# Four graph layers on one core: the ends of layer 3 rearranged, and their statistics and row scalings given to ScalarE

## The chip, the cores and the metric

The kernel runs on one core of a Trainium2 chip. A core has engines that run side by side, each with its own queue of instructions: TensorE (PE in the profile; loads of its weights are PEld) for matrix products, VectorE (DVE) for elementwise work and reductions, ScalarE (ACT) for functions of one argument, GpSimd (POOL), and SyncE (SP), whose queue issues most transfers. SBUF holds working data in 128 partitions; PSUM takes TensorE's results. The metric is the device time of one execution in microseconds (us), lower is better.

## The reference, cut to what matters

Input x is 16 batches of 1024 nodes with 64 features; adj is one 1024 x 1024 0/1 matrix for all batches. Four layers follow each other, each as a residual with a layer norm:

```python
x = _layernorm(x + _L0_gnn_ref(x, W, a, adj))              # attention with additive scores
x = _layernorm(x + _L1_gnn_ref(x, w0, b0, wa, ba, adj))    # softmax per feature over neighbours
x = _layernorm(x + _L2_gnn_ref(x, adj, W, a))              # as layer 0
x = _layernorm(x + _L3_gnn_ref(x, adj, Wh, bh, Wo, bo, gamma, beta))

# layer 3
mask = graph + eye(N) > 0
h = einsum('bnc,hdc->bhnd', x, Wh)                 # 4 heads of 64
scores = where(mask, einsum('...nd,...md->...nm', h, h), NEG)
out_h = softmax(scores) @ h + bh
z = leaky_relu(cat(out_h), 0.2)                    # 256 features
h2 = z @ Wo.T                                      # 64 features: the outer attention
out2 = softmax(where(mask, h2 @ h2.T, NEG)) @ h2 + bo
z2 = leaky_relu(out2, 0.2)
out = (z2 - mean) * rsqrt(var + 1e-5) * gamma + beta
```

So layer 3 ends, for each batch, in two layer norms: the inner one with gamma and beta, and the one of the residual.

## The kernel before

The nodes lie in 128 partitions times 8 chunks (C = 8). Layers 0 to 2 pass over the batches in turn. In layer 3 each batch has 32 **head units** and 8 **outer units**. A unit is one key chunk against 1024 queries: scores on TensorE into a PSUM tile, their exponential on ScalarE into a tile e, the mask on VectorE (e times the adjacency), the product of e with the values on TensorE. Head units work on two of the four heads at once (lines 1330 to 1354), pair n = 0 first and then n = 1, each with query halves h = 0 and 1. Outer units (lines 1486 to 1524) work on the single outer head; for them VectorE also adds up the masked rows (`add_up`, line 1499), except in the last batch, where `add_all` (line 1526) does it by matmuls with ones.

The units are grouped into **bursts** of five (`plan`, line 1998, and `run`, line 2011). Batch b has bursts 0 to 7; a burst holds five head units in bursts 0 to 3, and in bursts 4 to 7 three head units of b with two outer units of b - 1 between them. Batches are counted from 0 to 15, E = 15 is the last. For every burst `run` writes, in this order: finishing steps left over (`catch_up`), the scores and exponentials of its five units, the tasks listed under `mids`, the roots of pending variances (`roots`, on ScalarE), the products of the burst before (`drain`), the masks of this burst, the tasks listed under `slots`. The order on TensorE, ScalarE, VectorE and GpSimd is the order written (`manual_schedule`); SP's queue is ordered by the framework. Score tiles rotate through three PSUM buffers (`ps_s`); other PSUM results in layer 3 take turns in the same three. There are eleven buffers for e.

Tasks are put at (batch, burst) by `at`. The list at line 1917 places what follows the head units of a batch: projection of a pair's result (`project_T`), the reciprocal of its sums, which go through DRAM by SP's queue (`inverse`), the quotient and leaky ReLU (`quotient`); then the outer projection (`h_2T`, line 1443), the bound of its scores (`shift_of`, line 1268: norms by TensorE, maximum by VectorE, across partitions by GpSimd, to ScalarE's bias), its values (`h_2v`). After a batch's outer units come its **ends** (lines 1548 to 1666): `gather` turns the result and divides it by its sums, `layer` adds bo and applies the leaky ReLU, `mean`, `centre` and `scale` make the inner norm from sums, differences, squares and sums of squares over full-width tiles (128x512), all on VectorE; `affine` multiplies by the inverse root and gamma, `residual` adds beta and x, three more steps make the second norm, `finish` scales and stores. Roots are taken on ScalarE (logarithm and exponential, line 706) and improved by a step of three small VectorE instructions (line 710). Batch 14 takes its powers on GpSimd, its second squares on ScalarE (line 1636) and its last scaling row by row on ScalarE.

Elsewhere there is another form: `bn_stats` (eight instructions), `moments` (line 754: seven small instructions, then root, step and shift) and `scaled` (line 776), which scales eight chunks, one ScalarE instruction each:

```python
for c in rows:
    nc.scalar.activation(dst[:, c, :], src[:, c, :], AF.Identity,
        bias=shift[:, c : c + 1], scale=rstd[:, c : c + 1])
```

Layer 2 ends its batches so (`store`, line 1112). Its tasks have places of their own (lines 1130 to 1141); those at or after step `own` of the round behind its last batch are carried into the bursts of layer 3's batch 0, one per burst. In the round itself stand the eviction of the last batch's product, its projection, the division and, ahead of them, row scalings of batches 12 and 13.

After the last head units comes a serial stretch: the second pair of batch 15 is projected and divided (`project`, line 1399), turned (`z_T`, line 1437), projected (`h_2T`), and the 8 outer units of batch 15 run as burst 8; then sums, the quotient and two norms (`last_layer`, `last_quotient`, `last_norms`). Ten checks of value bounds (`known`, line 2033, `look`, line 2042) are written into this stretch; if a check fails a general path runs.

Of the kernel before, what the change touches and what calls it, by code (L numbers as in the profile page):

```python
# [8 lines left out]
F32 = mybir.dt.float32  # L9
# [7 lines left out]
P = 128  # L17
# [565 lines left out]
def fast_path(  # L583
# [316 lines left out]
    def gat_layer(w, name, zero_mean, own, room=None):  # L900
# [238 lines left out]
        for b in range(B):  # L1139
            for task, (t, k) in zip(work[b][2], ends[b % 2]):  # L1140
                at(b + t, k, task)
# [293 lines left out]
    def prep_out(b):  # L1435

        def z_T():
            pt = ps_s.tile([P, C, P], F32, tag="s", name="pzT")
            for c in range(C):
                nc.tensor.transpose(pt[:, c, :], zs[b][:, c, :], ident)  # L1440
            nc.scalar.copy(zTs[b][:, NP - 1, :], pt.rearrange("p c q -> p (c q)"))

        def h_2T():
# [5 lines left out]
            pt = one_bank("ph2T")  # L1449
            for n in range(NP):  # L1450
                for h in range(2):
                    nc.tensor.matmul(  # L1452
                        pt[h * D : (h + 1) * D, :], woT[:, n], zTs[b][:, n, h * HALF : (h + 1) * HALF],
                        start=(n == 0), stop=(n == NP - 1),
                    )
# [25 lines left out]
        return z_T, h_2T, h_2v, swap, biased  # L1481

    def head_out(b):
# [42 lines left out]
        def add_all():  # L1526
            t = ps_h.tile([P, HALF], F32, tag="acc0", name="u2")
            for k in range(C):
# [5 lines left out]
            held["u"] = l3.tile([P, HALF], F32, tag="y", name="u2T", bufs=1)  # L1534
            nc.scalar.copy(held["u"], t)

        def turned():
# [7 lines left out]
            held["tot"] = po[1][:, : 2 * CH].rearrange("p (j h) -> p j h", h=2)  # L1545
# [15 lines left out]
        def last_quotient():  # L1561
            total = sums[:, b, H, :]
            for j in range(CH):
# [44 lines left out]
        def layer():  # L1608
# [4 lines left out]
            held["n"] = normalizing(v, held["m"], b >= B - 2)  # L1613
# [6 lines left out]
        def residual():  # L1620
            m = held["m"]
            if b < B - 2:
                nc.vector.tensor_tensor(m, m, bc_mid(beta, C), ALU.add)
            nc.vector.tensor_tensor(m, m, xb(b), ALU.add)
            held["n"] = normalizing(m, held["v"], b >= B - 2)
# [10 lines left out]
        def squares():  # L1636

            m, sq = held["m"], held["v"]
            st = small.tile([P, C], F32, tag="ln_sum", name="ln_sum")
            nc.vector.tensor_reduce(st, m, AX.X, ALU.add)  # L1640
            held["less"] = small.tile([P, C], F32, tag="ln_mean", name="ln_mean")
            nc.vector.tensor_scalar(held["less"], st, -1.0 / D, None, ALU.mult)
            held["vs"] = small.tile([P, C], F32, tag="ln_vs", name="ln_vs")
            for c in range(C):
                nc.scalar.activation(
                    sq[:, c, :], m[:, c, :], AF.Square, bias=held["less"][:, c : c + 1],
                    accum_out=held["vs"][:, c : c + 1],
                )

        def power():  # L1650
            ve = small.tile([P, C], F32, tag="ln_ve", name="ln_ve")
            nc.vector.tensor_scalar(ve, held["vs"], 1.0 / D, LN_EPS, ALU.mult, ALU.add)
            held["rstd"] = small.tile([P, C], F32, tag="ln_rstd", name="ln_rstd")
            nc.gpsimd.tensor_tensor(held["rstd"], ve, neg_half, ALU.pow)

        def rows():
            shift = small.tile([P, C], F32, tag="ln_ve", name="ln_shift")
            nc.vector.tensor_tensor(shift, held["less"], held["rstd"], ALU.mult)
            res = ep.tile([P, C, D], F32, tag="m", name="res", bufs=4)
            scaled(res, held["m"], (held["rstd"], shift), range(C))  # L1660
# [10 lines left out]
        ends = [gather, layer, mean, centre, scale, affine, residual, mean, centre, scale, finish]  # L1671
# [434 lines left out]
```

## Time and profile before

| | |
|---|---|
| median of 3 runs | 1978.29 us (1972.04 to 1978.98) |
| profiled execution | 1970.04 us, span 1967.8 us |
| mean granted TensorE clock | 0.984 |
| busy: TensorE, VectorE, ScalarE, GpSimd | 1879.4, 1762.7, 1332.3, 83.0 us |
| layer 3: first scores, first scores of batch 1 | 649.75, 715.70 us |
| first scores of batch 14, of batch 15 | 1749.26, 1828.91 us |
| last mask of a head unit ends | 1918.9 us |
| outer masks of batch 15 | 1933.0 to 1942.2 us |
| first statistics of batch 15's norms | 1952.73 us |

Times are from the start of the span. A row of the order-of-time view gives start, duration, engine, line, operation, output and input tiles, shapes and count of merged instructions; in brackets the idle time before it and what ended that. A row's duration of several merged instructions is from the first start to the last end. "Granted clock" is the share of full speed that the throttle left to TensorE.

### The profile page before, as it was taken

How to read it: one execution, taken by the hardware profiler on the slowest of the kernel's cores; microseconds unless marked ns; L12 is line 12 of the kernel's file. 1: busy time of each engine (PE TensorE's matmuls, PEld its weight loads, DVE VectorE, ACT ScalarE, POOL GpSimd, SP SyncE). 2: the span in 40 equal slices, each digit the busy share in tenths (PEclk: the TensorE clock that was granted, in tenths of full speed). 3: DMA queues.
4: the chain of work that ended last, by engine and by line, in shares of the span. 5: the costliest groups of instructions: out<-in, count | busy, mean ns of one | idle time of the engine just before them, and what ended most of it. 6: DMA issues, size and time to landing. Idle time of an engine off the chain costs nothing.

```text
span 1967.8 us, 25841 instructions
## 1 busy us (share of the span) xinstructions
PE 1879.4 (96%) x9545; PEld 767.6 (39%) x9545; DVE 1762.7 (90%) x2963; ACT 1332.3 (68%) x2344; POOL 83.0 (4%) x77
## 2 busy tenths in 40 slices
PE   7999989989888899999999999999999999999985
PEld 4444437863333333333333333333333333333332
DVE  5899988879999777798999989999899898998997
ACT  5356567857667776667767767677666776776653
POOL 0000000000000000000000000000000000000001
PEclk8999999999999999999999999999999999999998
DMA  7000000000000120000000000000000100010000
GB/s 179 1 1 1 1 1 1 1 1 1 1 1 3 51 56 12 12 12 19 22 17 12 20 25 12 17 18 22 17 12 18 28 12 17 12 28 17 12 17 18
DMA packets 45748, 35.90 MB, mean 18 GB/s; under 512 B 37295, under 2 KB 37616, under 8 KB 45614
## 3 DMA queue, kind: packets, MB, share of 16 engines
q1 hardware_dynamic: 45310, 34.14, 6.7%
q8 instruction: 77, 1.26, 0.3%
q14 instruction: 57, 0.47, 0.1%
q10 hardware_dynamic: 304, 0.03, 0.0%
HBM read 29.45 MB, written 4.70 MB: 17 GB/s over the span
## 4 chain that ended last, share of the span: by engine, by line
PE 70%; DVE 22%; ACT 5%; issue 1%; DMA 1%; POOL 0%; SPq 0%; DVEq 0%; POOLq 0%; ACTq 0%
PE y L1351 19%; PE s L1336 19%; DVE e L991 7%; PE y_l L1003 6%; PE po L1833 5%; PE y L1516 4%; PE s L1491 4%; DVE e L1344 4%; PE u_l L1015 3%; DVE e L1509 2%; DVE junk L1501 1%; PE phT L1310 1%; ACT e L1340 1%; PE poT L1378 1%; PE ph2T L1452 1%
## 5 line engine op out<-in xcount | busy, mean ns | idle before, releaser
L1340 ACT ACTIVATE e<-s,shift 128x1024 f32<-128x1024 f32 x512 | 539.3, 1123 | 221.2 <-PE s L1336 221.2
L1344 DVE TENSOR_TENSOR e<-e,aT 128x1024 f32<-128x1024 f32 x512 | 596.4, 1215 | 12.9 <-ACT e L1340 12.9
L1336 PE MATMUL s<-hT 64*128 64x512 f32 x2048 | 491.6, 604 | 1.4 <-ACT hT L1319 0.9
L1351 PE MATMUL y<-e,vals 128*64 128x512 f32 x2048 | 485.6, 601 | 5.5 <-DVE e L1344 4.3
L991 DVE SCALAR_TENSOR_TENSOR e<-G_l,q,aT 128x1024 f32<-128x1024 f32 x256 | 315.4, 1275 | 6.4 <-ACT G_l L968 6.3
L1336 PEld LDWEIGHTS s<-hT 64*128 64x128 f32 x2048 | 183.5, 186 | 289.0 <-issue 149.6
L1003 PE MATMUL y_l<-e,vals_l 128*64 128x512 f32 x1024 | 254.2, 616 | 26.9 <-DVE e L991 20.1
L1351 PEld LDWEIGHTS y<-e,vals 128*64 128x64 f32 x2048 | 135.9, 137 | 273.5 <-issue 200.3
L1509 DVE TENSOR_TENSOR e<-e,aT 128x1024 f32<-128x1024 f32 x128 | 156.2, 1225 | 9.8 <-DVE junk L1501 0.5
L1501 DVE SCALAR_TENSOR_TENSOR junk<-e,aN 128x1024 bf16<-128x1024 f32 x120 | 146.1, 1218 | 0.0
L1496 ACT ACTIVATE e<-s,shift 128x1024 f32<-128x1024 f32 x128 | 138.4, 1114 | 0.4 <-PE s L1491 0.4
L1516 PE MATMUL y<-e,h2v 128*64 128x512 f32 x512 | 127.2, 599 | 0.9 <-DVE e L1509 0.9
L1491 PE MATMUL s<-h2T 64*128 64x512 f32 x512 | 125.8, 591 | 0.0
L1003 PEld LDWEIGHTS y_l<-e,vals_l 128*64 128x64 f32 x1024 | 62.3, 138 | 160.4 <-issue 75.7
L1833 PE MATMUL po<-hi,aR 128*128 128x512 f32 x256 | 102.7, 402 | 11.1 <-ACT hi L1762 7.3
L1279 POOL PARTITION_ALL_REDUCE gtop<-top x48 | 55.3, 1152 | 1268.7 <-DVE top L1277 970.0
L1833 PE MATMUL po<-lo,aR 128*128 128x512 f32 x256 | 101.0, 395 | 0.0
L780 ACT ACTIVATE x<-m,bn_shift,bn_rstd 128x64 f32<-128x64 f32 x256 | 88.5, 430 | 0.0
L1491 PEld LDWEIGHTS s<-h2T 64*128 64x128 f32 x512 | 50.0, 186 | 60.2 <-issue 37.3
L1383 ACT COPY zT<-poT 64x512 f32<-64x512 f32 x124 | 72.0, 581 | 1.3 <-PE poT L1378 0.2
L1516 PEld LDWEIGHTS y<-e,h2v 128*64 128x64 f32 x512 | 36.6, 138 | 76.4 <-issue 58.5
L978 ACT ACTIVATE vals_l<-x,p 128x64 f32<-128x64 f32 (+1 forms) x256 | 64.3, 339 | 0.0
(270 smaller groups left out, 1876.1 us busy)
## 6 DMA issues: line engine op xcount, KB each, us to landing
r<-inverse SPq DMA_DIRECT2D x62, 256.0 KB
adj<-in_adj_dram SPq DMA_DIRECT2D x16, 512.0 KB
x<-in_x_dram SPq DMA_DIRECT2D x16, 256.0 KB
out_dram<-res SPq DMA_DIRECT2D x15, 256.0 KB
rows<-yT SPq DMA_DIRECT2D x62, 4.0 KB
sums<-rows SPq DMA_DIRECT2D x31, 8.0 KB
inverse<-rt SPq DMA_DIRECT2D x31, 8.0 KB
out_dram<-res SPq DMA_DIRECT2D x2, 128.0 KB
```

Source lines behind the costliest of these rows:

```text
L991: nc.vector.scalar_tensor_tensor(e, G[b - b % 2][:, b % 2, :], pq[b - b % 2][1][:, k, b % 2 : b % 2 + 1], aT[:, k, :], ALU.max, ALU.mult,)
L1003: nc.tensor.matmul(held["y"][h * D : (h + 1) * D, :], vals[b][:, k, :], e[:, h * HALF : (h + 1) * HALF], start=(k == 0), stop=(k == C - 1),)
L1336: nc.tensor.matmul(s[:, i, :], hT[rows, k * P : (k + 1) * P], hT[rows, cols], start=True, stop=True)
L1340: nc.scalar.activation(e, s, AF.Exp, bias=shifts[b, n])
L1344: nc.vector.tensor_tensor(e, e, bc_mid(aT[:, k, h * HALF : (h + 1) * HALF], 2), ALU.mult)
L1351: nc.tensor.matmul(held[h][i * D : (i + 1) * D, :], vals[b][:, k, :], e[:, i, :], start=(k == 0), stop=(k == C - 1),)
L1491: nc.tensor.matmul(s[:, i, :], hT[rows, (i + k // CH) % 2, k % CH * P : (k % CH + 1) * P], hT[rows, 0, :], start=True, stop=True,)
L1496: nc.scalar.activation(e, s, AF.Exp, bias=shifts[b])
L1501: nc.vector.scalar_tensor_tensor(junk.rearrange("p c q -> p (c q)").bitcast(BF16), e.rearrange("p i q -> p (i q)"), 1.0, aN[:, k, :], ALU. ...
L1509: nc.vector.tensor_tensor(e, e, aT[:, k, :].rearrange("p (i q) -> p i q", i=2), ALU.mult)
L1516: nc.tensor.matmul(held["o"][h * D : (h + 1) * D, :], vals["out", b][:, k, :], e[:, h, :], start=(k == 0), stop=(k == C - 1),)
L1833: nc.tensor.matmul(po.rearrange("p q k f -> p (q k f)"), aR[:, k, ic * P : (ic + 1) * P], e[:, k].rearrange("p q k f -> p (q k f)"), start ...
```

## The change

Layer 2: batch 15's eviction moves one step forward, its projection, division and quotients follow at once, batch 12's row scaling moves behind them, and `own` is 2 instead of 6, so that the row scalings of batches 12 and 13 come into bursts 0 and 1 of layer 3's batch 0 and the six tasks behind them two bursts later than before.

Layer 3: in batches 14 and 15 bursts 4 to 7 hold 2, 2, 3 and 5 head units with 3, 3, 2 and 0 outer units of the batch before. The ends of batch 13 and 14 use `bn_stats`, `moments` and row scalings on ScalarE; they are placed as shown below. `rows_1` and `rows_2` write the step and the shift (VectorE) and at once the eight ScalarE instructions. beta is added to x for batches 13 to 15 beforehand. In the last stretch the transposed z is copied in halves, the first half of the outer projection (`part_2T(0)`) is written earlier, `add_all` is split around `last_layer` and batch 14's second norm, and the tile for the total gets a PSUM buffer of its own. Eight checks move into bursts 0 to 3 of batch 3, two stay at the end.

```diff
@@ layer 2
+            places = ends[b % 2]
+            if zero_mean and b == B - 4:
+                places = [*places[:-1], (4, 3)]
+            if zero_mean and b == B - 1:
+                places = [(1, 0), (1, 1), (1, 1), (1, 1), *places[4:]]
...
-    l2_ahead, l2_go = gat_layer(later["w2"], "l2", True, 6, room=dict(
+    l2_ahead, l2_go = gat_layer(later["w2"], "l2", True, 2, room=dict(
@@ z_T and h_2T
-            for c in range(C):
-                nc.tensor.transpose(pt[:, c, :], zs[b][:, c, :], ident)
-            nc.scalar.copy(zTs[b][:, NP - 1, :], pt.rearrange("p c q -> p (c q)"))
+            for h in range(2):
+                part = slice(h * CH, (h + 1) * CH)
+                for c in range(h * CH, (h + 1) * CH):
+                    nc.tensor.transpose(pt[:, c, :], zs[b][:, c, :], ident)
+                nc.scalar.copy(
+                    zTs[b][:, NP - 1, h * HALF : (h + 1) * HALF], pt[:, part].rearrange("p c q -> p (c q)")
+                )
...
+        def part_2T(n):
+            if n == 0:
+                held["p"] = one_bank("ph2T")
+            for h in range(2):
+                nc.tensor.matmul(
+                    held["p"][h * D : (h + 1) * D, :], woT[:, n], zTs[b][:, n, h * HALF : (h + 1) * HALF],
+                    start=(n == 0), stop=(n == NP - 1),
+                )
@@ ends
+        def stats_of(src, key):
+            st = small.tile([P, C, 6], F32, tag="bn2", name="bn2", bufs=2)
             for c in range(C):
+                nc.vector.bn_stats(st[:, c, :], src[:, c, :])
+            held["root"], held[key] = moments(st)
+            if b < B - 2:
+                roots.append(held["root"])
+        def layer_stats():
+            v = held["v"]
+            nc.vector.tensor_tensor(v, v, bc_mid(bo, C), ALU.add)
+            leaky(v, v)
+            held["m"] = ep.tile([P, C, D], F32, tag="m", name="m", bufs=4)
+            stats_of(v, "n1")
+        def root_1():
+            held["root"]()
+        def rows_1():
+            scaled(held["m"], held["v"], held["n1"](), range(C))
+        def residual_sum():
+            m = held["m"]
+            nc.vector.tensor_tensor(m, m, bc_mid(gamma, C), ALU.mult)
+            nc.vector.tensor_tensor(m, m, xb(b), ALU.add)
+        def residual_stats():
+            residual_sum()
+            stats_of(held["m"], "n2")
+        def residual_power():
+            residual_sum()
+            held["n2"] = statistics(held["m"])
+        def shifted():
+            mean, rstd = held["n2"]
             shift = small.tile([P, C], F32, tag="ln_ve", name="ln_shift")
+            nc.vector.scalar_tensor_tensor(shift, mean, -1.0, rstd, ALU.mult, ALU.mult)
+            held["n2"] = lambda: (rstd, shift)
+        def rows_2():
             res = ep.tile([P, C, D], F32, tag="m", name="res", bufs=4)
+            scaled(res, held["m"], held["n2"](), range(C))
             nc.sync.dma_start(out[b].rearrange("(p c) d -> p c d", c=C), res)
...
+        if b == B - 3:
+            ends = [gather, layer_stats, rows_1, residual_stats, rows_2]
         if b == B - 2:
-            ends[7:] = squares, power, rows
+            ends = [gather, layer_stats, root_1, rows_1, residual_power, shifted, rows_2]
@@ places
         if b == E - 2:
-            places[9:] = [(17, mids), *((j, slots) for j in (17, 17, 18, 18, 20, 20, 21, 22, 22, 24))]
+            places[9:] = [(16, mids), *((j, slots) for j in (16, 17, 18, 19))]
...
-        gather, work[E][1][1][1], layer, z_T, mean, centre, h_2T, lambda: shift_of(E, hTs[E][1]), swap, h_2v, scale,
-        lambda: look(known[:3]), biased,
+        gather, work[E][1][1][1], lambda: part_2T(0), layer_stats, z_T, lambda: h_2T(1), lambda: shift_of(E, hTs[E][1]),
+        root_1, swap, h_2v, biased,
     ):
         at(E, BURSTS - 1, task)
...
-        affine, residual, squares, lambda: look(known[3:]), power, add_all, last_layer, last_quotient, rows, last_norms,
+        lambda: add_all(0), last_layer, residual_power, lambda: add_all(1), lambda: look(known[8:]),
+        shifted, last_quotient, rows_2, last_norms,
     ):
         at(E, BURSTS, task)
-    for b in (E - 1, E):
-        at(E, 2, lambda b=b: nc.vector.tensor_tensor(xb(b), xb(b), bc_mid(beta, C), ALU.add))
+    at(E, BURSTS, rows_1, mids)
+    at(E - 1, 1, lambda: nc.vector.tensor_tensor(xb(E - 1), xb(E - 1), bc_mid(beta, C), ALU.add))
+    at(E - 1, 2, lambda: nc.vector.tensor_tensor(xb(E - 2), xb(E - 2), bc_mid(beta, C), ALU.add))
+    at(E, 1, lambda: nc.vector.tensor_tensor(xb(E), xb(E), bc_mid(beta, C), ALU.add))
+    for j in range(4):
+        at(3, j, lambda j=j: look(known[2 * j : 2 * j + 2]))
@@ units of a burst
-            n = 5 if j < 4 else 3
+            n = (2, 2, 3, 5)[j - 4] if b >= E - 1 and j >= 4 else 5 if j < 4 else 3
...
+            m = 5 - n
+            for i, unit in enumerate(outer[:m]):
+                burst.insert(1 + (2 - j % 2) * i if m == 2 else (1, 3, 4)[i], unit)
+            outer = outer[m:]
```

## The prediction

> **What bounds the kernel now.** I read the shares by engine first.
>
> ```profile
> PE 1879.4 (96%) x9545; PEld 767.6 (39%) x9545; DVE 1762.7 (90%) x2963; ACT 1332.3 (68%) x2344; POOL 83.0 (4%) x77
> ```
>
> TensorE is nearly always occupied. Layer 3 is therefore bound by TensorE as long as its matmuls find their operands, and a change at the ends counts where they do not. So I followed the chain that ended last through the final 130 us; its shares by line begin:
>
> ```profile
> by line: DVE e L1344 21.9%; DVE e L1509 14.5%; DVE junk L1501 7.2%; issue 3.7%; DVE flags L2031 2.9%; POOL last_rstd L1587 2.5%; DVE ln_vs L736 2.1%; DVE ok L2030 2.0%; DVE zT L1396 1.9%; DVE zT L786 1.9%; DVE m L1624 1.6%; DVE bn L1577 1.6
> ```
>
> Here it is VectorE's masks (lines 1344 and 1509) and sums (1501), not matmuls. The order-of-time view says where the two meet. I write (15,2) for batch 15, burst 2. TensorE:
>
> ```profile
> 1848.67 4.56 PE L1336 MATMUL s<-hT 64*128 64x512 f32 x20
> ...
> 1906.49 1.08 PE L1351 MATMUL y<-e,vals 128*64 128x512 f32 x4
> 1911.92 1.98 PE L1351 MATMUL y<-e,vals 128*64 128x512 f32 x4 [4.34 <-DVE e L1344]
> ...
> 1918.34 1.88 PE L1351 MATMUL y<-e,vals 128*64 128x512 f32 x8
> ```
>
> The scores of (15,2), then a first true wait of 4.34 us: TensorE is packed until 1907.6 and only (15,7)'s products wait for VectorE. VectorE has no gap from 1806.5 to 1918.9, when its last mask ends; TensorE's last product ends at 1920.2. Packed, it would have ended at 1907.6 plus 4.4 for five products, 1912. So TensorE has 8.3 us to give away in batch 15, VectorE nothing. Last, ScalarE beside VectorE:
>
> ```profile
> 1839.02 5.14 ACT L1340 ACTIVATE e<-s,shift 128x1024 f32<-128x1024 f32 x5 [0.47 <-PE s L1336]
> ...
> 1849.85 5.13 ACT L1340 ACTIVATE e<-s,shift 128x1024 f32<-128x1024 f32 x5 [3.13 <-PE s L1336]
> ```
>
> ```profile
> 1846.28 5.70 DVE L1344 TENSOR_TENSOR e<-e,aT 128x1024 f32<-128x1024 f32 x5
> ...
> 1868.44 5.76 DVE L1344 TENSOR_TENSOR e<-e,aT 128x1024 f32<-128x1024 f32 x5
> ```
>
> ScalarE's exponentials of (15,1) end at 1844.2, VectorE's masks of the same burst at 1852.0: VectorE runs 7.8 us behind, in burst 3 8.5 us (exponentials to 1865.7, masks 1868.44 to 1874.2). Each engine takes its instructions in the order written. A ScalarE instruction that needs something VectorE does after a burst's masks waits out that lag, with the next burst's exponentials queued behind it.
>
> **The start of layer 3.** Rows of ScalarE, then TensorE:
>
> ```profile
> 644.78 2.74 ACT L780 ACTIVATE x<-m,bn_shift,bn_rstd 128x64 f32<-128x64 f32 x8
> 647.43 0.56 ACT L1022 COPY yT_l<-y_l 128x512 f32<-128x512 f32 x1
> ...
> 652.82 5.12 ACT L1340 ACTIVATE e<-s,shift 128x1024 f32<-128x1024 f32 x5
> ...
> 700.42 2.76 ACT L780 ACTIVATE x<-m,bn_shift,bn_rstd 128x64 f32<-128x64 f32 x8
> ```
>
> ```profile
> 704.37 0.34 PE L1273 MATMUL pn<-pair_ones,hsq 128*128 128x2 bf16 x8 [1.14 <-ACT e L1340]
> ...
> 706.86 3.40 PE L1351 MATMUL y<-e,vals 128*64 128x512 f32 x8 [1.14 <-ACT yT L1358]
> ```
>
> Batch 12's row scaling (8 instructions, 2.74) stands ahead of the eviction that the last projection of layer 2 needs; batch 15's, at 700.42, holds the exponentials of (0,6) and costs TensorE 1.1 and 1.1 of waiting and one stretch at half clock, in which 8 matmuls take 3.40 instead of 1.7. Moved: eviction at 644.8, projection done by about 647, quotients some 3.3 us earlier. But batch 12's scaling (2.76) then lies ahead of (0,1)'s exponentials, so 0.5 of it stays; batch 13's goes into ScalarE's 2.68 gap ahead of (0,2). Batch 14's and 15's scalings go to bursts 6 and 7: of the 4.1 us lost I leave 1.0 (the eviction of y still comes late) and 0.6 (the scaling ahead of (1,0)). Sum -0.4 - 2.5 = **-2.9**, between -4.5 (all of it and the 0.4) and 0 (the losses come back one burst later). TensorE is packed from there to batch 15, so this arrives.
>
> **Checks in batch 3.** Eight checks, by their rows at the end 0.7 each for the four wide ones, 0.53 for two, 0.36 for two: 4.6 on VectorE. In batch 3 it idles 2.87 at 899.5 (for the outer projection) and 1.75 at 910.4 (for the norms): **0**. Without that cover: at most 4.6. The earlier beta additions (0.7 each, bursts 1 and 2 of batch 14) fall ahead of gaps of 0.81 and 2.38 there: 0.
>
> **Batch 14's outer units** earlier: VectorE gets 1.26 more in bursts 4 and 5 and 2.5 less in 7. The norm reduction of 1817.84 comes up to 2.5 later, ScalarE's exponentials of (14,7) 1 us later; VectorE stands 6.3 us behind ScalarE in (15,0) and does not notice: 0 (at most 1).
>
> **Batch 15, the main term.** Removed from VectorE before its last mask: batch 13's sums, centrings, squares and scalings, 12.3 plus 1.3 of beta; added: gather 0.9, twice 3.7 (two full-width operations at 0.72, eight statistics 1.10, seven small ones 1.2), twice a step and shift at 0.8, beta 0.65: 10.55. VectorE alone gains 3.05. But rows_1 and rows_2 put eight scalings (2.76 by line 780) on ScalarE in (15,1) and (15,3), each behind a step on VectorE that follows that burst's masks. Chain, in times of the old trace:
> - Masks of (15,1) end at 1852.0 + 3.7 (layer_stats) = 1855.7; batch 12's variance 1.1, step and shift 0.8: 1857.6. Rows 2.76: 1860.4. The first exponential of (15,2) ends at 1861.5, not 1850.95. VectorE has 3.1 of other work (quotient, beta) meanwhile and idles 0.8.
> - Three score buffers are free, so TensorE does three units of (15,2) and stands from 1851.3 to 1861.5: 10.2, of which it has 8.3.
> - Masks of (15,2) to 1867.2, residual_stats 3.7, swap 0.9: 1871.8. TensorE does two scores 1.8, five products 4.45, the outer projection 1.8, five scores 4.5 and norms 0.25: 1874.3, plus half clock after the standstill. By these rows that costs half its length:
>
> ```profile
> core 0: us, PE busy (x) PEld busy (x) DVE busy (x) ACT busy (x) POOL busy (x), PEclk, DMA share, GB/s
> 649.75:652.30 2.55, 2.08 (x5) 0.51 (x4) 0.38 (x2) 2.52 (x12) 0.00 (x0) 0.59 0.01 3
> 1911.90:1914.30 2.40, 1.98 (x4) 0.30 (x4) 2.37 (x4) 0.00 (x0) 0.00 (x0) 0.50 0.00 0
> 1916.70:1918.30 1.60, 1.58 (x4) 0.48 (x6) 1.60 (x2) 0.00 (x0) 0.00 (x0) 0.54 0.00 0
> ```
>
> One stretch lost 1.7 at 706.4; the one from 1911.4 to 1918.2 was twice as long but waiting for masks anyway. I take 1.7 (0 to 3.4): norms at 1876. VectorE has idled 4.3.
> - Masks of (15,3) to 1882.0, step and shift 1882.8, rows 1885.6, first exponential of (15,4) 1886.9. Nothing else is written for VectorE there: 4.1 idle.
> - (15,4): 2 x 1.14 + 3 x 2.40 = 9.5, to 1896.4; finish 0.6; then the reciprocal waits for its sums, whose transfer stands behind that finish's output on SP's queue (2.37 from the finish's end in batch 14; affine and residual used to fill it): 2.4, 0.2: 1899.6. (15,5) 9.5, quotient 2.5, (15,6) 8.2, projection 2.0, (15,7) 5.7: 1927.5, against 1918.9. **+8.6**, less 0.1 as the last product follows a shorter mask.
> Batch 13's output is issued on SP (0.37) in (15,3), before the pair's rows and sums need that queue: 0. GpSimd loses one power (2.14 at 1935.92, off the path).
>
> TensorE counted alone agrees: 1912 + 10.2 + 4.1 + 1.7 = 1928 for its last product. Bounds: -3 if ScalarE is never held, +13.7 with full half clocks at both standstills.
>
> The clock, by a page: "TensorE: Matmul & The Clock Gate" (Part 1) has half rate after about 3.4 us of idleness until a window of 3.4 us is busy. The case agrees in size, but at 706.4 two waits of 1.1 sufficed, and after 1911.4 a window 70% busy did not end it. By the page alone the second standstill adds 1.7 too, and the main term would be an estimated +10.3.
> Against the change speaks "ScalarE: Activation LUTs" (Rules for kernel authors): multiply and add belong on VectorE. Its budget of 0.3 us plus 0.83 ns per element makes eight rows 2.83 by estimate; the sum would be 0.1 more.
>
> **Gap and tail.** From the last z (1924.0) to the last exponentials: copying the transposed z in halves saves 0.45 of 1.01; layer_stats on VectorE (3.7) delays the norm by 0.3: -0.15. The checks and step that leave (1929.9 to 1933.0) held the masks 1.5 us, but the products are bound by TensorE (1936.62 plus 7.09) behind the same score pace: 0. After the last product (1943.7), 9.0 us passed to the first statistics (1952.73). Now add_all(0) 1.8, transposes 0.7, copy 0.6, leaky 0.7; VectorE stands idle for this copy some 6 us, because leaky is written ahead of residual_power; then 1.4, statistics 1.1 and 1.0; the power on GpSimd 2.2 with two checks (1.75) beneath; shift 0.2, sums, reciprocal and quotient 1.3: 11.1. **+2.1**; the end is unchanged.
>
> Sum: -2.9 + 8.5 + 2.0 = +7.6. The profiled execution took 1970.04 (span 1967.8 and 2.2 around it), 8.25 below the median: 1977.6 for such a one, **1985.9** against the median of 1978.29.
>
> **Rivals.** (a) ScalarE is not held: the variances would have to be there before ScalarE finishes the same burst, the lags of 7.8 and 8.5 be gone. Then -3.05 + 2.0 - 2.9 = -4, 1974. For it: 8 rows are only 2.76 in bursts where ScalarE idles 3 us; against it: the step is written behind the masks. (b) Clearly slower: half clock twice as long at the first standstill and also at the second, +3.4, and no gain at the start, +2.9: 1989 to 1993. For it: the long stretch of 1911.4; against it: score pace after a standstill is ScalarE's 1.0 a unit, not TensorE's. (c) TensorE's 8.3 us are all won: -8.3 + 2 - 2.9 = -9.2, 1969; it needs VectorE faster by 8 where only 3 are removed.
>
> **How the numbers follow.** Forecast, with the sums' transfer covered or not and the start worth 1 to 4: 1981 to 1988, 0.58. (b) 0.24, (a) 0.15, (c) 0.03. A measurement tells 0.5%, 9.9 us. Faster needs (c) and a little more: 0.03. Slower is (b) and the forecast's upper edge, 0.24 + 0.06. Same 0.67. The range leaves out half of (a) and the top of (b): 1974 to 1993; the forecast's own is 1981 to 1988.
>
> **What would show it.** ScalarE's rows of line 780's helper in (15,1) and (15,3) with idle time ahead, released by VectorE's shift; exponentials behind them; TensorE waiting for an exponential for about 10 and 4 us, granted clock below 1 after; VectorE idle some 4 us ahead of (15,4) and 6 us ahead of the last leaky; at the start, no waits at 704 to 707. If those ScalarE waits are absent, the main term is wrong; if VectorE's gaps are there but the end moved less than 3 us, some work ran in an order other than written.

## The result and the profile after

The changed kernel takes 1981.24 us (median), the kernel before, run beside it, 1971.9 us: a ratio of 1.0039, with a 95% interval of 1.0022 to 1.0055. By this ratio it is 7.7 us more (4.3 to 10.8), by the two medians alone 9.3; the forecast had 7.6 more. Differences in the times below go by the ratios. The forecast of 1985.9 stood on a median before of 1978.29, which this comparison found 6 us lower. The profiled execution has a span of 1977.6 us (before: 1967.8).

The shares by engine, in the page of the kernel after:

```profile
PE 1882.7 (95%) x9545; PEld 769.9 (39%) x9545; DVE 1759.2 (89%) x3002; ACT 1341.6 (68%) x2355; POOL 80.6 (4%) x76
```

Nothing in this line gives the loss away: VectorE has 3.5 us less to do than before, ScalarE 9.3 more, TensorE 3.3 more with the same 9545 matmuls (they ran longer, at half clock). The chain of the kernel before has no counterpart to show, since the chain of the profile after breaks off at the last norm; the order of time has to do. TensorE after, in order of time (start, duration, engine, line, operation, number of instructions, and in brackets the idle time ahead and what ended it):

```profile
1847.83 2.85 PE L1341 MATMUL s<-hT 64*128 64x512 f32 x12
1859.46 3.78 PE L1341 MATMUL s<-hT 64*128 64x512 f32 x8 [8.79 <-ACT e L1345]
...
1885.94 3.68 PE L1507 MATMUL s<-h2T 64*128 64x512 f32 x8 [3.46 <-ACT e L1345]
...
1922.44 5.43 PE L1356 MATMUL y<-e,vals 128*64 128x512 f32 x24
...
1936.42 9.08 PE L1507 MATMUL s<-h2T 64*128 64x512 f32 x32
...
1952.45 1.92 PE L1549 MATMUL u<-e,ones 128*32 128x512 f32 x16
```

The second row is the loss. Before, TensorE was packed through (15,2); now three units of (15,2) are done at 1850.68, and it stands 8.79 us until an exponential (line 1345) frees a score buffer. It stands again for 3.46 us in (15,4). Its last head products end at 1927.87, before at 1920.2. The last two rows are the scores of batch 15's second output and its first row sums. ScalarE after:

```profile
1855.49 2.78 ACT L780 ACTIVATE m<-v,bn_shift,bn_rstd 128x64 f32<-128x64 f32 x8 [7.21 <-DVE bn_shift L771]
1858.29 3.13 ACT L1345 ACTIVATE e<-s,shift 128x1024 f32<-128x1024 f32 x3
...
1881.93 2.77 ACT L780 ACTIVATE res<-m,bn_shift,bn_rstd 128x64 f32<-128x64 f32 x8 [4.67 <-DVE bn_shift L771]
```

The engine that frees the buffers is itself idle: 7.21 and 4.67 us ahead of the eight row scalings (line 780), because it waits for `bn_shift`, a 0.17 us instruction on VectorE. The exponentials stand directly behind. VectorE after:

```profile
1848.07 5.70 DVE L1349 TENSOR_TENSOR e<-e,aT 128x1024 f32<-128x1024 f32 x5
...
1855.29 0.17 DVE L771 SCALAR_TENSOR_TENSOR bn_shift<-bn_mean,bn_rstd 128x8 f32<-128x8 f32 x1
...
1871.26 0.42 DVE L1482 COPY h2T<-h2T 64x512 f32<-64x512 f32 x1 [2.19 <-ACT h2T L1476]
...
1875.38 0.17 DVE L1282 TENSOR_REDUCE top<-pn 128x1 f32<-128x8 f32 x1 [2.68 <-PE pn L1278]
...
1885.92 1.23 DVE L1349 TENSOR_TENSOR e<-e,aT 128x1024 f32<-128x1024 f32 x1 [4.03 <-ACT e L1345]
...
1898.61 0.25 DVE L1392 RECIPROCAL rt<-sums 128x16 f32<-128x16 f32 x1 [2.30 <-DMA sums<-rows]
...
1955.62 0.69 DVE L786 SCALAR_TENSOR_TENSOR v<-v 128x512 f32<-128x512 f32 x1 [6.38 <-ACT v L1576]
...
1962.75 1.11 DVE L1596 BATCH_NORM_STATS2 bn<-v 128x6 f32<-128x64 f32 x8
```

The shift that ScalarE waits for (1855.29) stands behind the masks of (15,1), which begin at 1848.07. The rows behind it say what the late exponentials then cost VectorE: 2.19, 2.68 and 4.03 us idle, where it had no gap at all before. The 2.30 at 1898.61 is a wait for the transfer of the sums. The last two rows are the tail: 6.38 us idle ahead of the leaky step that waits for ScalarE's copy, then the first statistics of the last norm. TensorE at the start of layer 3:

```profile
660.03 3.17 PE L1341 MATMUL s<-hT 64*128 64x512 f32 x8 [2.51 <-ACT e L1345]
663.14 4.98 PE L1356 MATMUL y<-e,vals 128*64 128x512 f32 x20
...
704.77 1.94 PE L1356 MATMUL y<-e,vals 128*64 128x512 f32 x8 [0.69 <-ACT yT L1363]
...
716.04 2.13 PE L1341 MATMUL s<-hT 64*128 64x512 f32 x8 [1.05 <-ACT e L1345]
```

The waits of 1.14 and 1.14 us at 704 to 707 are down to 0.69, but a new one of 2.51 us stands at 660, in (0,1), and the eight matmuls behind it take 3.17 us instead of 2, the twenty after them 4.98 instead of 4.51. Last, the granted clock (PEclk) by stretches:

```profile
core 0: us, PE busy (x) PEld busy (x) DVE busy (x) ACT busy (x) POOL busy (x), PEclk, DMA share, GB/s
...
1859.00:1862.00 3.00, 2.54 (x6) 1.18 (x8) 2.56 (x3) 2.83 (x4) 0.00 (x0) 0.50 0.02 5
1862.00:1865.00 3.00, 3.00 (x10) 0.59 (x8) 2.63 (x3) 2.13 (x4) 0.00 (x0) 0.50 0.00 0
1865.00:1868.00 3.00, 3.00 (x16) 1.02 (x14) 2.93 (x11) 0.59 (x1) 0.00 (x0) 0.90 0.00 0
1885.90:1889.30 3.40, 3.36 (x8) 1.26 (x9) 3.27 (x4) 3.11 (x3) 0.00 (x0) 0.53 0.12 44
1937.00:1940.80 3.80, 3.80 (x13) 3.00 (x11) 2.49 (x6) 2.51 (x4) 0.00 (x0) 0.55 0.00 0
```

Half clock holds for some 6 us of work after the first standstill, once more after the second, and again in the last scores, which took 9.08 us for 32 matmuls (7.72 before).

Where the difference lies, stretch by stretch, from the starts of the same instructions in the traces. The first column is where layer 2's last product starts; what lies ahead of it is the same code in all kernels and still ends between 642.9 and 651.4, so spans of single executions can't be compared to better than that, while the other columns can.

| Kernel | layer 2's last product starts | from there to the first score of (15,0) | from there to batch 15's last head product | from there to the end |
|---|---|---|---|---|
| before | 644.19 | 1184.72 | 90.71 | 48.2 |
| after | 642.94 | 1185.41 | 98.94 | 50.3 |
| A: scalings a burst later | 651.43 | 1187.00 | 87.17 | 49.1 |
| B: batch 13's ends as before | 642.90 | 1184.99 | 90.56 | 49.3 |
| C: start alone | 649.06 | 1184.29 | 91.81 | 48.2 |
| D: tail order | 648.67 | 1186.39 | 98.49 | 46.5 |
| E: units repeated | 644.30 | 1183.93 | 97.67 | 49.0 |
| F: start, tasks spread | 644.30 | 1178.83 | 91.92 | 48.2 |
| G: A + D | 644.74 | 1185.85 | 87.17 | 46.2 |
| H: A + D + spread | 644.47 | 1179.76 | 87.18 | 47.5 |
| I: H, two outer units each | 643.19 | 1179.69 | 88.07 | 47.6 |
| J: H, first shift one place earlier | 647.63 | 1180.38 | 86.44 | 46.2 |

Batch 15 alone has 8.2 of the loss, the end 2.2, all that lies ahead of batch 15 0.7; together 11.1, of which 1.25 are missing in the span since the layers ahead ran that much shorter in this execution.

### The profile page after: what moved, and what is told of

Its sections match the earlier page's. It is cut to its first block, busy times and chain, and to the rows that moved or that the text cites. A ratio compares the mean times of both kernels' runs of the same rounds, so it can differ in the third digit from the quotient of the medians.

```text
span 1977.6 us, 25877 instructions
## 1 busy us (share of the span) xinstructions
PE 1882.7 (95%) x9545; PEld 769.9 (39%) x9545; DVE 1759.2 (89%) x3002; ACT 1341.6 (68%) x2355; POOL 80.6 (4%) x76
## 5 line engine op out<-in xcount | busy, mean ns | idle before, releaser
L1363 ACT COPY yT<-y 128x512 f32<-128x512 f32 x64 | 38.5, 602 | 43.8 <-PE y L1356 41.8
```

## The experiments

The theory: ScalarE, which takes its instructions in order, is held by scalings whose shift VectorE makes only behind a burst's masks. Rivals: the scalings, sixteen instructions that VectorE's wide ones did before, are simply too much for ScalarE; or the new share of outer units (3, 3, 2, 0) is to blame.

**A, shift and scalings taken apart.** All of the change stays; the step and shift become tasks of their own. The first shift stays behind the masks of (15,1), and its scalings move one burst later, behind the exponentials of (15,2). The residual's statistics move two bursts later, the second scalings three.

```diff
+        def step_1():
+            done = held["n1"]()
+            held["n1"] = lambda: done
...
-            ends = [gather, layer_stats, rows_1, residual_stats, rows_2]
+            ends = [gather, layer_stats, step_1, rows_1, residual_stats, step_2, rows_2]
...
-            places[9:] = [(16, mids), *((j, slots) for j in (16, 17, 18, 19))]
+            places[9:] = [(16, mids), (16, slots), (18, mids), (18, slots), (20, slots), (22, mids), (22, slots)]
```

> All of the change stays. Only batch 13's own ends are taken apart: the shift that VectorE makes for the row scalings becomes a task of its own, queued several score units ahead of the eight ScalarE activations that use it, so that the scalings find it done. Theory 1 (ScalarE, in order, is held by the scalings waiting for VectorE's shift behind the masks, and the exponentials behind them come late): the two waits of the changed kernel, 7.21 us ahead of the first scaling and 4.67 us ahead of the second, fall below 1 us; TensorE's waits of 8.79 us in batch 15's outer units and 3.46 us in its second scores go; about 8 us come back, so the time is 8 us below the changed kernel and near the kernel before (ratio to before 0.998 to 1.002). Theory 2 (the amount of ScalarE's work counts, sixteen activations of 0.35 us that VectorE had before): the same 5.6 us of scalings are still there, the time stays within 2 us of the changed kernel (ratio 1.003 to 1.005). Theory 3 (the outer units moved to three, three, two and none cost it): the same as theory 2, with the waits ahead of the scalings gone and TensorE's standing in another place.

Measured: 1970.24 us, ratio to before 0.9992 (0.9982 to 1.0003), 9.3 us below the changed kernel. ScalarE in this kernel, in order of time, around the first scalings:

```profile
1859.08 5.13 ACT L1345 ACTIVATE e<-s,shift 128x1024 f32<-128x1024 f32 x5 [0.72 <-PE s L1341]
...
1868.59 2.76 ACT L780 ACTIVATE m<-v,bn_shift,bn_rstd 128x64 f32<-128x64 f32 x8 [2.77 <-DVE bn_shift L771]
1871.26 0.56 ACT L1476 COPY h2T<-ph2T 128x512 f32<-128x512 f32 x1
1871.86 0.63 ACT L1477 ACTIVATE h2sq<-h2T 128x512 bf16<-128x512 f32 x1
1872.39 5.12 ACT L1345 ACTIVATE e<-s,shift 128x1024 f32<-128x1024 f32 x5
```

TensorE of the same kernel beside it:

```profile
1868.56 1.99 PE L1341 MATMUL s<-hT 64*128 64x512 f32 x8
1871.88 1.13 PE L1341 MATMUL s<-hT 64*128 64x512 f32 x4 [1.33 <-ACT h2T L1476]
1873.54 2.13 PE L1341 MATMUL s<-hT 64*128 64x512 f32 x8 [0.54 <-ACT e L1345]
```

The scalings still take 2.76 us and ScalarE still waits 2.77 ahead of them (and 1.69 ahead of the second ones; neither wait falls below 1). But the exponentials of (15,2), at 1859.08, now stand ahead of the wait and not behind it, and TensorE's 8.79 is down to 1.33 and 0.54. The shift itself is not earlier: counted from the first score of batch 15 it ends at 30.1 us, in the changed kernel at 27.1. What changed is what queues behind the wait. Batch 15 takes 87.17 us, 11.8 less than in the changed kernel with the same amount of work on ScalarE and the same outer units. Both rivals fall. How the 11.8 divide between the two groups of scalings and the moved statistics was not measured. It is also 3.5 us less than before: the change's rearrangement has a gain of that size, which the held exponentials buried.

**B, batch 13's ends as before,** its addition of beta included.

```diff
-        if b == B - 3:
-            ends = [gather, layer_stats, rows_1, residual_stats, rows_2]
...
-            places[9:] = [(16, mids), *((j, slots) for j in (16, 17, 18, 19))]
+            places[9:] = [(17, mids), *((j, slots) for j in (17, 17, 18, 18, 20, 20, 21, 22, 22, 24))]
...
```

> All of the change but one part: batch 13's ends are computed and placed as in the kernel before (mean, centre and scale on VectorE, the shift added there, no row scalings on ScalarE). Theory 1 (batch 13's scalings cost the main term): the last head products of batch 15 end about 8 us earlier than in the changed kernel, at 1920 us from the start of the span; what is left over the kernel before is the tail (about 2 us, 9.0 to 11.1 us from the last product to the first statistics) and the outer units less the start's gain, together +0 to +3 us over the kernel before (ratio 1.000 to 1.0015). Theory 3 (the new share of outer units, three, three, two and none, costs it): the time stays near the changed kernel, ratio 1.003 to 1.005.

Measured: 1973.57 us, ratio 1.0008 (0.9997 to 1.0019), as the theory had it; batch 15 takes 90.56 us, before 90.71. So the outer units' new share is not the cause: batch 14 is some 0.7 us longer (from the first score of (14,0) to that of (15,0), in A, B and the changed kernel alike; TensorE waits 0.52 us there for the exponentials of (14,7)), and batch 15 pays nothing. It gains nothing there either. TensorE of this kernel at the end of batch 15 waits for VectorE's masks just as before, 4.34 us:

```profile
1912.24 6.80 PE L1356 MATMUL y<-e,vals 128*64 128x512 f32 x20 [4.34 <-DVE e L1349]
```

**C, the start alone**, in the kernel before: the new places in layer 2 and `own` 2.

```diff
...
-    l2_ahead, l2_go = gat_layer(later["w2"], "l2", True, 6, room=dict(
+    l2_ahead, l2_go = gat_layer(later["w2"], "l2", True, 2, room=dict(
```

> The kernel before with the start alone: the places of the last batches' ends in layer 2 and the first two input projections of layer 3 ahead instead of six. Everything else as before. The forecast's own term says 2.9 us less than before (bounds 4.5 to 0). A second reading of the changed kernel's trace, with the two kernels aligned on layer 2's last product, says 0.8 us less: the first exponentials of layer 3 now stand behind batch 12's scaling on ScalarE, and TensorE still waits 2.5 us for them. Ratio to before 0.9985 by the forecast, 0.9996 by the second reading; a loss would say that the start was bought with a later wait.

Measured: 1971.92 us, ratio 0.9997 (0.9986 to 1.0007). The interval reaches from 2.8 us of gain to 1.4 of loss and does not hold the forecast's 2.9; the trace has 0.4 us of gain up to (15,0). TensorE in (0,1) of this kernel:

```profile
666.12 3.79 PE L1341 MATMUL s<-hT 64*128 64x512 f32 x8 [2.50 <-ACT e L1345]
```

**F, the start with the carried tasks spread**: C, and the eight tasks that layer 2 carries into batch 0 placed so that no scaling lies ahead of the first exponentials.

```diff
-    for j, task in enumerate(ending):
+    for j, task in zip((1, 3, 0, 1, 2, 3, 4, 6), ending):
         at(0, j, task)
```

> The kernel before with the change's start, and the eight tasks that layer 2 carries over into layer 3's first batch given new places: the scaling of batch 12 goes one burst later, the shift and scaling of batch 13 three bursts later and those of batches 14 and 15 to bursts 4 and 6, so that no scaling stands on ScalarE ahead of the first exponentials. The start alone gave a ratio of 0.9997 (0.9986 to 1.0007). Theory (the start's gain went into TensorE's 2.50 us wait for exponentials that stand behind batch 12's scaling of 2.8 us, and into the half clock after it): that wait and the half clock's 1.7 us go, together with the later ones of 0.7 to 1.1 us, and the time is 5 to 7 us below the kernel before (ratio 0.9965 to 0.9975). Rival (the carried scalings cost the same wherever they stand, ScalarE or VectorE is short in the whole first batch): the wait moves to another burst, ratio 0.999 to 1.001.

Measured: 1966.12 us, ratio 0.9963 (0.9949 to 0.9977), by the ratio 7.3 us less than before; the second column of the table has 5.9 us less. TensorE in the same place:

```profile
657.74 3.15 PE L1341 MATMUL s<-hT 64*128 64x512 f32 x12 [0.88 <-ACT hT L1324]
```

Twelve matmuls behind a wait of 0.88, which the kernels before and C have there too, and none for an exponential, where the kernel of C waits 2.50 and goes on at half clock. The start's edit was worth more than forecast, but only with the scalings out of the way.

**D, the tail's order.**

```diff
-        lambda: add_all(0), last_layer, residual_power, lambda: add_all(1), lambda: look(known[8:]),
+        residual_power, lambda: look(known[8:]), lambda: add_all(0), last_layer, lambda: add_all(1),
```

> All of the change, but with the last tasks after batch 15's products in another order: the residual's sum and power of batch 14 and the last known bounds stand ahead of the first half of the row sums and of the last layer's leaky step, which waits for ScalarE's copy. Theory (VectorE's wait of 6.38 us ahead of the leaky step is open time that the residual work queued behind it could have filled; its place is the cause of the 2 us of tail): from the last product to the first statistics of the last norm it takes about 7.4 us instead of 10.3 to 11.1, the time is 3 to 4 us below the changed kernel. Rival (the tail is bound by TensorE's sums and ScalarE's copy): the statistics start at the same time within 0.5 us and the kernel's time stays.

Measured: 1980.18 us, ratio 1.0044 (1.0032 to 1.0056): by the times, no gain. By the trace there is one. VectorE in the tail:

```profile
1954.89 0.69 DVE L1677 TENSOR_TENSOR m<-m,gamma 128x512 f32<-128x512 f32 x1 [0.48 <-ACT m L780]
...
1960.53 0.69 DVE L786 SCALAR_TENSOR_TENSOR v<-v 128x512 f32<-128x512 f32 x1 [0.49 <-ACT v L1576]
...
1963.52 0.17 DVE L1586 COPY sums<-tot 128x8 f32<-128x8 f32 x1 [2.23 <-PE tot L1583]
...
1964.69 1.11 DVE L1596 BATCH_NORM_STATS2 bn<-v 128x6 f32<-128x64 f32 x8
```

The residual's work fills the wait of 6.38 us, and the statistics of the last norm start at 1964.69, 7.33 us after the first row sum (1957.36 on TensorE); in the changed kernel it is 10.30 (1952.45 to 1962.75). The comparison and the trace disagreed, so the edit was tried again on kernel A.

**G, A and D together.**

> The changed kernel with batch 13's shift made ahead of its scalings (which alone gave a ratio of 0.9992) and the tail's order with the residual's power first. The tail order alone showed 7.3 us from the last product to the first statistics where the changed kernel has 10.2, but its median had not fallen with it. Theory (the 2.9 us are real, and the median of that comparison was taken with too few undisturbed executions to show them): ratio to before 0.9975 to 0.998. Rival (what VectorE gains is lost again at the end of the span): 0.999 to 1.000.

Measured: 1967.26 us, ratio 0.9968 (0.9951 to 0.9986), 4.7 us below A's ratio, with 2.9 us less in the last column of the table. The two intervals overlap (A reaches down to 0.9982, G up to 0.9986), so that the gain of the tail's order is shown by the traces and only supported by the times. Why D's median had not fallen stays open: its six executions lie in two groups of three (1977.8 to 1978.1 and 1982.3 to 1983.4), and in the profiled one layer 2 ends 5.7 us later than in that of the changed kernel (first column of the table), more than the gain.

**E, the clock.** One score unit of (15,2) is computed nine times, so that TensorE works through most of the standstill.

```diff
-            for i in range(2):
-                rows = slice(i * D, (i + 1) * D)
-                nc.tensor.matmul(
-                    s[:, i, :], hT[rows, k * P : (k + 1) * P], hT[rows, cols], start=True, stop=True
-                )
+            for _ in range(9 if (b, n, h, k) == (B - 1, 0, 1, 4) else 1):
+                for i in range(2):
+                    rows = slice(i * D, (i + 1) * D)
+                    nc.tensor.matmul(
+                        s[:, i, :], hT[rows, k * P : (k + 1) * P], hT[rows, cols], start=True, stop=True
+                    )
```

> All of the change, and one score unit of batch 15 (the third of the burst behind which TensorE stands 8.79 us) is computed nine times over into the same bank, 7.7 us of the same products more: the outputs stay the same and TensorE is at work for most of the standstill instead of idle. It prices the clock by itself. In the changed kernel the half clock after that standstill lasts some 10 us of the span, and eight score products take 3.78 us where a warm row has 1.99. Theory 1 (the half clock after the standstill is paid in full by the end): the products behind take their warm durations and the time is 1.7 to 3 us below the changed kernel. Theory 2 (VectorE's masks set the pace behind the standstill, a slower TensorE is hidden): the durations are warm again but the last head products end at the same time within 0.5 us, and the time stays.

Measured: 1981.8 us, ratio 1.0046 (1.0030 to 1.0061), no gain in the times. TensorE of this kernel (its lines below 1341 are one further down):

```profile
1847.70 9.71 PE L1342 MATMUL s<-hT 64*128 64x512 f32 x44
1859.33 3.08 PE L1342 MATMUL s<-hT 64*128 64x512 f32 x8 [1.91 <-ACT e L1346]
...
1884.53 3.47 PE L1508 MATMUL s<-h2T 64*128 64x512 f32 x8 [3.44 <-ACT e L1346]
```

The granted clock of the same kernel by stretches:

```profile
core 0: us, PE busy (x) PEld busy (x) DVE busy (x) ACT busy (x) POOL busy (x), PEclk, DMA share, GB/s
1855.00:1859.00 4.00, 2.42 (x12) 0.78 (x8) 3.35 (x5) 3.61 (x9) 0.00 (x0) 1.00 0.01 2
1859.00:1862.50 3.50, 3.17 (x10) 0.97 (x12) 3.19 (x3) 3.33 (x5) 0.00 (x0) 0.68 0.00 0
1862.50:1867.00 4.50, 4.50 (x20) 1.45 (x22) 4.43 (x10) 1.96 (x4) 0.00 (x0) 0.87 0.00 0
```

The repetition kept TensorE at work up to 1857.41, but the 1.91 us that were left of the standstill brought a new half clock, from these rows 1.1 and 0.6 us lost, a stretch of 3.4. In the changed kernel the rows from 1859 on lose 1.5, 1.5 and 0.3, a stretch of 6.6. So 1.6 us of lost clock went, and batch 15 is 1.3 us shorter in the trace; two kernels with the same batch 15 (the changed one and D) differ by 0.45 there. The times can't resolve it. Neither theory is met as written, since the half clock was only halved; the trace leans to the first: what the clock loses there is paid for the greater part. All of it, 3.3 us, would be less than half of the 8.2.

**H, the three edits together** (A, D and the spread of F), made since each part was worth something.

> The changed kernel with three edits together: batch 13's shift ahead of its scalings, the tail's order, and the carried tasks of layer 2 spread over the first batch of layer 3. By the sum of the parts (1.5 us below before, 2.9 of the tail, 5 to 7 of the start) 9 to 11 us below the kernel before, ratio 0.994 to 0.9955. If the spread start gives nothing, it is at the time of the kernel that has only the other two edits.

Measured: 1960.88 us, ratio 0.9938 (0.9914 to 0.9961): 12.2 us below the kernel before, somewhat more than the 9 to 11 expected, and 20 below the changed one. Two variations of it follow.

**I, batch 15's outer units two to each burst again.**

```diff
-            n = (2, 2, 3, 5)[j - 4] if b >= E - 1 and j >= 4 else 5 if j < 4 else 3
+            n = (2, 2, 3, 5)[j - 4] if b == E - 1 and j >= 4 else 5 if j < 4 else 3
```

> The kernel with the three edits together (ratio to before 0.9938, 0.9914 to 0.9961), but in batch 15 the outer units go two to each of the bursts 4 to 7, as before, instead of three, three, two and none; batch 14 keeps the new share. It prices the share itself, now that no scaling holds ScalarE. Theory 1 (the share is worth nothing of its own either way, TensorE, ScalarE and VectorE have the same work): within 1.5 us of that kernel, ratio 0.993 to 0.9947. Theory 2 (the share is a gain: with two units in the last burst TensorE waits some 4.3 us for VectorE's masks at the end of batch 15 as in the kernel before): 3 to 5 us more, ratio 0.9955 to 0.9965.

Measured: 1960.95 us, ratio 0.9935 (0.9912 to 0.9958), like H; batch 15 is 0.9 us longer in the trace. The share has next to no price of its own either way.

**J, the first shift one place earlier than in H,** and its scalings too, still behind the exponentials of (15,2).

```diff
-            ... (18, mids), (18, slots), (20, slots), (22, mids), (22, slots)]
+            ... (17, slots), (18, mids), (20, slots), (22, mids), (22, slots)]
```

> The kernel with the three edits together, and batch 13's first shift one place earlier still, behind the masks of burst 1 of batch 15, its scalings in the middle of burst 2. In that kernel ScalarE still waits 2.76 us for this shift, and TensorE 1.33 and 0.54 us behind it for the copy and the exponentials that stand after the scalings. Theory (these waits are on the path): they go, and the time is 1 to 2 us lower, ratio 0.993 to 0.9935. Rival (VectorE sets the pace there, its masks run without a gap across that place): the waits go and the time stays within 0.5 us, ratio about 0.9938.

Measured: 1960.39 us, ratio 0.9930 (0.9907 to 0.9953). The waits of 1.33 and 0.54 are gone and batch 15 is 0.7 us shorter, between what theory and rival expected; the times can't tell it from H. TensorE's wait for an exponential in (15,7) grew from 1.65 to 2.55 us in return. ScalarE of this kernel:

```profile
1848.65 5.14 ACT L1345 ACTIVATE e<-s,shift 128x1024 f32<-128x1024 f32 x5 [0.73 <-PE s L1341]
1855.14 2.76 ACT L780 ACTIVATE m<-v,bn_shift,bn_rstd 128x64 f32<-128x64 f32 x8 [1.35 <-DVE bn_shift L771]
```

J says what A left open. Its first shift ends 27.1 us after the first score of batch 15 (1828.00), and its scalings start at once, at the very moment of the changed kernel. For these scalings only the exponentials of (15,2) have changed sides; the statistics of the residual and the second scalings stand as in A and H. Batch 15 is 12.5 us shorter than in the changed kernel.

## Why the prediction was right, and where it was not

**The main term held, step by step.** Forecast +8.5, measured +8.2 (98.94 against 90.71).
- "The first exponential of (15,2) ends at 1861.5, not 1850.95": its mask starts at 1859.44, so the exponential ended at about 1859.4, with (15,2) starting 0.8 us earlier in this trace. The rows waited 7.21 for the shift, the lag of 7.8 that the trace of before showed between ScalarE's exponentials and VectorE's masks.
- TensorE's standstills, forecast 10.2 and 4.1, were 8.79 and 3.46. VectorE's gaps, forecast 0.8, 4.3, 4.1 and 2.4, were 0.99, 4.87 (2.19 and 2.68, for the outer projection and the norms), 4.03 and 2.30. The last mask ended at 1926.7, forecast 1927.5.
- Kernels A and J show the cause itself and not only its traces: the same instructions, with the scalings behind the exponentials of (15,2) instead of ahead of them, and 11.8 and 12.5 us of batch 15 are gone. The lag of the shift remains in both; it costs little where nothing urgent is queued behind it. The forecast's rival (a), "ScalarE is not held", priced VectorE's relief at 3.05 us; A has 3.5 less than before. So the rival had about the right number for a kernel that the change was not.
- "I take 1.7 (0 to 3.4)" for the clock was low: after the first standstill the half clock lost some 3.3 us instead of 1.7, and after the second, where the forecast had none, it came as well (0.53 from 1885.9). E's trace suggests that some 1.3 of the first is paid. The standstills, 1.4 and 0.6 us shorter than forecast, made up for it.

**The start was mis-sized.** "Sum -0.4 - 2.5 = -2.9" came to -0.8 in the changed kernel's trace, counted from layer 2's last product.
- The -0.4 failed in the step "so 0.5 of it stays", which sets the scaling's 2.76 us against a start that comes 3.3 earlier and puts nothing on the clock. The first score did come 3.2 earlier, and TensorE does wait 2.51 us for the exponentials that batch 12's scaling (2.81 us, at 656.17) holds. But the matmuls behind that wait lose 1.65 us more at half clock (3.17 instead of 1.99 and 4.98 instead of 4.51), and the scores of (0,2) start 0.8 us later than before, not 0.4 earlier (in C 1.95 later, with 2.8 lost at half clock).
- The -2.5 came to -1.6. The "4.1 us lost" are about 3.7 in the rows of before (1.14, 1.14, and 3.40 against the 1.94 of the same eight matmuls in the kernel after), and batch 15's scaling left another wait of 1.05 at 716.

C measures the term at -0.6 us (-2.8 to +1.4); by the traces batch 2 starts at the same time in C as before. F shows that the forecast looked at the right place: spread, the same edit is worth 7.3 by the times and 5.9 by the trace.

**Checks in batch 3, forecast 0,** cost nothing: measured against the kernel before, the first score of (3,0) and that of (4,0) stand 2.07 and 2.06 us earlier in the changed one. VectorE's gaps of 2.87 and 1.75 us there shrank to 0.20 and 0.52, as the forecast had it. Batch 14's outer units, forecast 0 (at most 1), cost 0.7.

**Gap and tail, forecast +2.0.** From the last head product to the scores 0.2 less (forecast 0.15); from the first row sum to the statistics 10.30 against 9.10, +1.2, where the forecast had 2.1. The place and the reason were right (VectorE idle 6.38, forecast 6; D fills it), the size was not. The forecast let residual work, two statistics and the power follow the leaky step one after another, and that sum was 0.9 too long; no new wait was found.

**What the forecast did not have:** the 32 scores of batch 15's second output took 9.08 instead of 7.72 us at half clock, after the gap between the heads and the output in which TensorE runs only in short pieces. It is in the table's last column with 1.35 us. It is no property of the change: H and I have it (9.07 us), A, B, D, E, G and J, with the same instructions there, don't (7.72 or 7.73). C and F, with the tail of the kernel before, have it too (9.15 and 9.07), and there the last column is not longer for it (48.2 in both, as before).

So the traces differ by 11.1 us behind layer 2, the forecast said 7.6: of the 3.5 between, 2.1 are the start, 0.7 the outer units of batch 14, 1.35 the clock in the last scores, and 0.8 lie in batches 2 to 13 (0.66 of it in one step ahead of batch 10, where the change has nothing; A and D have steps of 0.4 and 0.6 there as well, C none). The tail (0.9), batch 15 (0.3) and the end with the gap (0.25) go the other way. The times agree with the forecast better (7.7 by the ratio) than its terms do, and the agreement to a tenth is luck; by the medians the difference is 9.3.

## What to carry to other kernels

When work moves to an engine with time to spare, follow each of its operands back: if one is made by an engine that runs 7 us behind, the idle engine inherits those 7 us, and so does everything that is queued behind it. Write the consumer a stage behind its small producer (here four instructions of 0.2 us), and write each group of long instructions behind the urgent ones that are due, not ahead. With that, the start's tasks spread and the tail reordered, the edit that lost 0.4% wins 0.6% here. And price a new wait with the half clock that can stand behind it: here 1.65 us behind a wait of 2.51.

## What the runs showed of the hardware

The same wait does not always cost the same clock. The wait of 2.50 us in (0,1) stands in seven of these kernels with the same instructions around it; the eight matmuls behind it took 3.08, 3.08, 3.08, 3.17, 3.78, 3.78 and 3.79 us, where eight warm ones take 1.99. In the kernel before, two waits of 1.14 us were followed by half clock, in E one of 1.91 us; in A waits of 1.33 and 0.54, and one of 1.65, were not. In the last scores it came in five of the twelve kernels (9.07 to 9.15 us against 7.72 or 7.73). So the length of a wait alone does not decide.

The Trainium skill, "TensorE: Matmul & The Clock Gate" (Part 1), says that the clock is granted by a window of about 3.4 us that runs freely, and goes to half after an idle window. That a wait's place against such a window decides would fit these numbers; it was not tested. Waits of 1.1 to 2.5 us sufficed here, less than an idle window of that length, and the measurement decides.
